# Layer 1's attention: the third and fourth rows of probabilities turned in 32x32 blocks by VectorE and DMA, and values multiplied in blocks of 128 columns, a head later

## The chip, the cores and the metric

The kernel runs on one core of a Trainium2 chip. The metric is the device time of one execution in microseconds. The kernel before takes 2954.98 us (median of three runs, 2953.38 to 2958.42). The engines are named as in the profile: PE (TensorE, matrix products), PEld (its weight loads, which overlap PE), DVE (VectorE), ACT (ScalarE), POOL (GpSimd) and SP (SyncE, which here only issues DMAs). Each engine works through its own list of instructions in order, and waits on semaphores for the others.

## The reference, cut to what matters

Four layers run one after the other, each the sum of an attention-like and a feed-forward part, on 4 sequences of 512 tokens with 256 features. The change lies in the attention of layer 1, a latent attention with 16 heads:

```python
q = _rmsnorm(x @ wq_a, q_a_ln_w) @ wq_b
q_nope, q_pe = (q[..., :D_NOPE], q[..., D_NOPE:])
compressed_kv, k_pe = (ckv[..., :KV_LORA], ckv[..., KV_LORA:])
...
scores = jnp.einsum('bqhd,bkhd->bhqk', qf, kf) * softmax_scale
scores = jnp.where(causal[None, None], scores, jnp.finfo(scores.dtype).min)
attn = jax.nn.softmax(scores, axis=-1)
out = jnp.einsum('bhqk,bkhd->bqhd', attn, v)
return out.reshape(b, s, N_HEADS * D_V) @ wo
```

The mask is causal: of a head's 4 x 4 blocks of 128 queries by 128 keys, ten are computed, one in the first row of blocks, four in the last.

## The kernel before

Layer 1 is one generator, `latent_pieces`, woven with three others: the product-key layer (`product_key_pieces`, with its gathers on POOL), the gated units of the feed-forward part, and the start of the next layer. `weave` takes at each turn the piece that is least advanced by the costs the generators yield; the Tile scheduler then sets the order of the instructions on each engine, and semaphores and buffers follow from that order. Where the code says `keep_in_program_order`, the scheduler keeps the instructions of that engine as they are written.

The weights are folded so that keys and values of all heads are the same 64 latent columns (`cv`) and a head's query has 128 rows: 64 latent ones and 64 rotated ones. There are 64 heads in all (4 sequences by 16), numbered `s`; two make a pair `p = s // 2`. A pair's queries come from `queries` (L1049 to L1074): four matmuls, ScalarE copies of the results, and four DMAs on SP (L1068) that copy the rotary half `pes` into `psw` with its 32-row parts exchanged. `rotate` (L1075 to L1080) then multiplies by cosines and sines and adds, on VectorE, into `qf`.

For each head, and each row i of 128 queries:

- `exp_scores` (L964): one matmul of (i + 1) x 128 columns into a PSUM bank of the tag `mm` (four banks; L971); VectorE adds the mask and finds the row's extreme (L974); ScalarE takes the exponential and the row's sum (L978). The result is the tile `pr0` to `pr3`, of two buffers each.
- At the third and fourth row VectorE inverts the sums (L1094) and ScalarE scales the rows, three at once and then the last (L1096).
- `turned` (L1098, matmuls L1103): for the head before, column block j of all rows from j on is transposed by PE into a PSUM bank of the tag `tr` (two banks), 4, 3, 2 and 1 blocks; VectorE copies even j, ScalarE odd j, into `PT` (L1107), which holds 1280 columns.

After the second head of a pair has been turned, `z` (L1239) is computed: for each column block j and both heads one matmul with `cv` as weights (64 columns, so that the two heads fill two halves of PE's columns) and 512, 384, 256 or 128 columns of `PT`. ScalarE scales `z` into `zT` (L1245), and every second pair two PSUM banks of outputs are formed (L1253) and added to x by VectorE (L171).

In layer 3's attention (`full_attention`), rows are already turned otherwise: VectorE transposes within 32x32 blocks (`turn_blocks`, L1581), four DMAs write the strips to memory (L1586), one reads them back in the final order (L1590), and the values are multiplied in blocks of 128 columns (L1625). Its rows in the profile are therefore rows for the same operations.

Of the kernel before, what the change touches and what calls it, by code (L numbers as in the profile page):

```python
# [16 lines left out]
P = 128  # L17
NB, SEQ, DM = 4, 512, 256
NT = NB * SEQ
NTILE = NT // P  # L20
TPB = SEQ // P
# [9 lines left out]
class Ctx:  # L31


    def __init__(self, tc, stack):
# [8 lines left out]
        self.trickle = []  # L43
# [8 lines left out]
    def unit(self, src, kept=lambda ins: ins):  # L52

        w = self.tile(self.weights, [P, 3072], "wu")
        kept(self.nc.sync.dma_start(w[:, : src.shape[1]], src))
        return w

# [942 lines left out]
def latent_pieces(c, a, keep, open_pool):  # L1000
# [4 lines left out]
    nc, tc = c.nc, c.tc  # L1005
    QL, KL = 192, 64
# [68 lines left out]
    def rotate(pes, psw, qf):  # L1075
        pec = c.tile(pool, [P, SEQ], "pec", bufs=1)
        nc.vector.tensor_mul(pec, pes, cosq)
        tc.keep_in_program_order(nc.vector.tensor_mul(psw, psw, sinq))
        nc.vector.tensor_add(qf[:KL, 1, :], pec[:KL, :], psw[:KL, :])
        nc.vector.tensor_add(qf[KL:, 0, :], pec[KL:, :], psw[KL:, :])  # L1080

    def probabilities(s, i):
        p, h = s // 2, s % 2
        b = p // 2 % 4
        if i == 0:
# [3 lines left out]
            c, pool, late, qfs[p][:, h, :], kf[:, h, b * SEQ : (b + 1) * SEQ], i, rinv[:, i : i + 1]  # L1089
# [8 lines left out]
    def turned(s, j):  # L1098

        pt = c.ps("tr")  # L1100
        n = SEQ - j * P
        for i in range(j, TPB):
            nc.tensor.transpose(  # L1103
                pt[:, (i - j) * P : (i - j + 1) * P], prs[s][i][:, j * P : (j + 1) * P], c.ident
            )
        copy = nc.scalar.copy if j % 2 else nc.vector.tensor_copy
        return lambda: copy(PTs[s][:, START[j] : START[j] + n], pt[:, :n])  # L1107

    START = (0, 512, 896, 1152)
# [5 lines left out]
    def latents(b):  # L1115

        if b < 2:
            rooms = [c.tile(pool, [P, 1280], "PT")[:, :1024]]
        elif b == 2:
            rooms = [c.tile(pool, [P, SEQ], "zT", bufs=3) for _ in range(2)]  # L1120
# [38 lines left out]
    for b in range(NB):  # L1159
        tokens = slice(b * SEQ, (b + 1) * SEQ)  # L1160
        lats.append(latents(b))
        for t in range(TPB):
# [5 lines left out]
            sq = c.tile(pool, [P, QL + KL], "pr1")  # L1168
# [12 lines left out]
        rot = c.tile(pool, [P, SEQ], "pr3")  # L1181
# [22 lines left out]
    copy = None  # L1204
    yield 1.9
    for s in range(65):
        if s < 64:
            prs[s] = []
        for i in range(TPB):
            if s < 64:  # L1210
                probabilities(s, i)
            if s > 0:
                if i == 0:
                    PTs[s - 1] = c.tile(pool, [P, 1280], "PT")
                ready, copy = copy, turned(s - 1, i)
                if ready:
                    ready()
            if i == 0 and s % 2 == 1 and s < 63:
                rotate(*turning)
            yield 0.85  # L1220
            if i == 1 and s % 2 == 0 and s < 62:
                turning = queries(s // 2 + 1)
                yield 2.6
        if copy:
            copy()
            copy = None
        if s > 0:
            del prs[s - 1]
        if s % 2 == 1:
            continue  # L1230
        if s == 0:
            continue

        p = s // 2 - 1
        g, b, pair = p // 8, p // 2 % 4, p % 2
        z = c.ps("acc")
        for j in range(TPB):
            for h in range(2):
                tc.keep_in_program_order(nc.tensor.matmul(  # L1239
                    z[h * KL : (h + 1) * KL, j * P :], lhsT=cv[:, b * TPB + j, :],  # L1240
                    rhs=PTs[s - 2 + h][:, START[j] : START[j] + SEQ - j * P],
                    start=(j == 0), stop=(j == TPB - 1),
                ))
        zTs[pair] = c.tile(pool, [P, SEQ], "zT", bufs=3)
        nc.scalar.mul(zTs[pair], z, kv_w)  # L1245
        yield 2.1
        if pair == 1:
            wz = weights[g][4]
            for t in range(0, TPB, 2):
# [10 lines left out]
                yield 1.7  # L1260

# [133 lines left out]
def layer1(c, a, xn, following):  # L1395


    with ExitStack() as stack, ExitStack() as right:
# [7 lines left out]
        latent = latent_pieces(c, a, keep, lambda: pool_of("l_h", 2))  # L1406
# [985 lines left out]
```

## Time and profile before

| | us |
|---|---|
| median of 3 runs | 2954.98 |
| the profiled execution | 2964.84 |
| its span, first to last instruction | 2962.9 |
| PE busy in the span | 2901.4 (98%) |
| DVE busy | 2136.9 (72%) |
| ACT busy | 1391.0 (47%) |
| layer 1's heads, about | 852 to 1482 |

The busy time of PE counts a matmul from its start to its modelled end; matmuls are pipelined, so successive ones overlap and the step from one start to the next is shorter than the duration shown. A matmul of 32-bit floats leaves two records, a transpose one. "Idle before" is the time for which an engine waited ahead of a group's instructions, with what ended the wait. A long idle time of an engine other than the bound costs nothing by itself. DMA rows give the median time from issue to landing.

### The profile page before, as it was taken

What the parts mean: (1) busy time and instruction counts of PE and PEld (TensorE: products, weight loads), DVE (VectorE), ACT (ScalarE), POOL (GpSimd) and SP (SyncE); (2) the same over time, 40 slices, a digit from 0 to 9 for tenths busy, and PEclk for the clock granted to TensorE, in tenths of its full rate; (3) what the DMA queues carried; (4) which work ended last, traced back from release to release, by engine and by line L of the source; (5) the groups of instructions that cost most, each with busy time, mean ns of one, the idle gap of its engine ahead of it and who ended that gap; (6) DMA issues with size and microseconds to landing.
All of it is one profiled execution on the core that took longest, in us unless ns stands there. A gap on an engine that the chain in (4) does not pass through costs nothing.

```text
span 2962.9 us, 40601 instructions
## 1 busy us (share of the span) xinstructions
PE 2901.4 (98%) x13812; PEld 1958.1 (66%) x13812; DVE 2136.9 (72%) x5434; ACT 1391.0 (47%) x3336; POOL 856.4 (29%) x681
## 2 busy tenths in 40 slices
PE   8999999999999999999999999999999999999999
PEld 5566666666755655555677678888888756666666
DVE  5877778787788788878666877777677666666656
ACT  4444445454376666667624554454454233333332
POOL 0565665656410033332043200000000033333331
PEclk9999999999999999999999999999999899999999
DMA  3333332332320134434244444444444300000000
GB/s 128 104 102 119 101 106 95 108 124 73 113 67 17 54 108 125 119 98 101 81 123 139 138 123 118 137 130 131 130 125 137 102 1 22 22 22 22 22 1 29
DMA packets 138366, 268.03 MB, mean 90 GB/s; under 512 B 19664, under 2 KB 99040, under 8 KB 133808
## 3 DMA queue, kind: packets, MB, share of 16 engines
q1 hardware_dynamic: 123696, 217.65, 23.5%
q0 software_dynamic: 14176, 47.01, 6.2%
q8 instruction: 109, 1.79, 0.2%
q14 instruction: 97, 0.79, 0.1%
q10 hardware_dynamic: 288, 0.79, 0.1%
HBM read 202.21 MB, written 54.26 MB: 87 GB/s over the span
## 4 chain that ended last, share of the span: by engine, by line
PE 81%; DVE 8%; ACT 3%; DMA 3%; POOL 1%; issue 1%; SPq 0%; ACTq 0%; DVEq 0%; POOLq 0%
PE mm L315 15%; PE mm L147 15%; PE mm L971 7%; PE acc L315 6%; PE tr L315 5%; PE acc L1625 5%; PE acc L987 4%; PE tr L809 3%; PE mm L155 2%; PE acc L1239 2%; PE acc L225 2%; PE tr L225 2%; PE acc L787 2%; PE acc L1253 2%; PE tr L1103 2%; DMA PT<-turned 1%
## 5 line engine op out<-in xcount | busy, mean ns | idle before, releaser
L978 ACT ACTIVATE pr<-pr,nm 128x128 f32<-128x128 f32 (+3 forms) x512 | 286.2, 559 | 334.8 <-DVE nm L974 332.7
L974 DVE CUSTOM_DVE_ANT_0 pr<-mm,late 128x128 f32<-128x128 f32 (+3 forms) x512 | 246.3, 484 | 79.0 <-PE mm L971 75.3
L147 PE MATMUL mm<-xnT,wu 128*128 128x512 f32 x624 | 289.1, 601 | 0.0
L326 ACT COPY part<-mm 128x512 f32<-128x512 f32 (+1 forms) x372 | 176.8, 479 | 198.1 <-PE mm L315 189.1
L315 PE MATMUL mm<-token_sums,unit_sums 128*128 128x512 f32 (+1 forms) x624 | 267.7, 512 | 2.1 <-ACT part L326 1.4
L1357 POOL DMA_INDIRECT e<-in_p_experts,ids x128 | 130.0, 1016 | 465.4 <-DVE x L165 325.1
L147 PE MATMUL mm<-xnT,w_in 128*128 128x512 f32 x512 | 229.2, 593 | 0.6 <-DVE cy L577 0.6
L477 DVE SCALAR_TENSOR_TENSOR x<-acc,cw,x 128x128 f32<-128x128 f32 x372 | 128.8, 346 | 107.4 <-PE acc L315 105.9
L577 DVE SCALAR_TENSOR_TENSOR cy<-mm,ws,cy 128x509 f32<-128x509 f32 (+2 forms) x216 | 160.2, 744 | 51.7 <-ACT cy L573 47.7
L147 PEld LDWEIGHTS mm<-xnT,wu 128*128 128x128 f32 x624 | 115.9, 193 | 118.7 <-issue 110.7
L971 PE MATMUL mm<-k,q 128*128 128x128 f32 (+3 forms) x512 | 175.2, 447 | 6.1 <-DVE q L1525 3.4
L971 PE MATMUL mm<-kf,qf 128*128 128x128 f32 (+3 forms) x512 | 173.8, 442 | 3.9 <-DVE qf L1080 3.6
L747 POOL TENSOR_TENSOR G<-G,CB 128x1024 f32<-128x1024 f32 x64 | 151.5, 2367 | 82.7 <-DVE G L710 76.6
L730 ACT ACTIVATE xD<-xc,ws 128x128 f32<-128x128 f32 x256 | 83.9, 390 | 192.7 <-POOL y L771 183.4
L315 PEld LDWEIGHTS acc<-down_sums,hidden_sums 128*128 128x128 f32 x744 | 112.1, 192 | 85.1 <-issue 83.2
L147 PEld LDWEIGHTS mm<-xnT,w_in 128*128 128x128 f32 x512 | 96.5, 190 | 104.4 <-issue 94.9
L1625 PEld LDWEIGHTS acc<-PT,V 128*128 128x128 f32 x1280 | 153.9, 194 | 13.6 <-DMA PT<-turned 9.4
L1625 PE MATMUL acc<-PT,V 128*128 128x128 f32 x1280 | 156.2, 278 | 5.0 <-DMA PT<-turned 4.8
L261 POOL TENSOR_TENSOR down_sums<-wu 128x256 f32<-128x256 f32 x8 | 6.1, 757 | 534.2 <-DMA turned<-Y 425.8
L710 DVE TENSOR_TENSOR_SCAN G<-G,eye 128x1024 f32<-128x1024 f32 x64 | 148.2, 2315 | 0.0
L460 DVE TENSOR_TENSOR whole<-mm,part 128x512 f32<-128x512 f32 x128 | 88.6, 692 | 68.4 <-PE mm L315 67.5
L1103 PEld LDWEIGHTS tr<-con,pr 128*128 128x128 f32 x640 | 79.7, 142 | 82.8 <-issue 20.0
(437 smaller groups left out, 6757.4 us busy)
## 6 DMA issues: line engine op xcount, KB each, us to landing
turned<-Y SPq DMA_DIRECT2D x252, 160.0 KB, 2.6
PT<-turned SPq DMA_DIRECT2D x63, 640.0 KB, 3.9
G<-own SPq DMA_DIRECT2D x64, 512.0 KB, 4.2
w_in<-in_m_units SPq DMA_DIRECT2D x16, 1024.0 KB, 4.9
eb<-since SPq DMA_DIRECT2D x96, 128.0 KB, 3.2
wu<-in_o_units SPq DMA_DIRECT2D x6, 1536.0 KB
wo<-in_m_units SPq DMA_DIRECT2D x16, 512.0 KB, 12.8
psw<-pes SPq DMA_DIRECT2D x128, 64.0 KB, 2.9
```

The costliest lines, as they stand in the source:

```text
L147: c.nc.tensor.matmul(out, lhsT=w[:, d, cols], rhs=c.xnT[:, d, tokens], start=(d == 0), stop=(d == 1))
L315: self.c.tc.keep_in_program_order(self.c.nc.tensor.matmul(bank, lhsT=lhsT, rhs=rhs, start=first, stop=True, skip_group_check=not first))
L326: self.c.nc.scalar.copy(r, bank)
L577: nc.vector.scalar_tensor_tensor(y[:, j:], src[:, : SEQ - j], conv[:, k, 3 - j : 4 - j], y[:, j:], ALU.mult, ALU.add,)
L710: tc.keep_in_program_order(nc.vector.tensor_tensor_scan(flat, flat, eye.rearrange("p h t -> p (h t)"), 0.0, ALU.mult, ALU.add))
L747: nc.gpsimd.tensor_mul(G, G, seqs[b][2][:, t, :][:, None, :].to_broadcast([P, HG, P]))
L971: kept(nc.tensor.matmul(sc, lhsT=q[:, i * P : n], rhs=k[:, :n], start=True, stop=True))
L974: nc.vector.tensor_tensor_reduce(out=pr, in0=sc, in1=late[:, SEQ - n :], scale=scale, scalar=-NEG, op0=ALU.add, op1=ALU.min, accum_out=nm,)
L978: nc.scalar.activation(pr, pr, AF.Exp, bias=nm, scale=-1.0, accum_out=total)
L1103: nc.tensor.transpose(pt[:, (i - j) * P : (i - j + 1) * P], prs[s][i][:, j * P : (j + 1) * P], c.ident)
L1357: nc.gpsimd.indirect_dma_start(out=e, out_offset=None, in_=a["p_experts"], in_offset=bass.IndirectOffsetOnAxis(ap=ids[:, t, k : k + 1], ax ...
L1625: kept(nc.tensor.matmul(zs[:, i], lhsT=head["V"][:, j, h, :], rhs=head["PT"][:, :, i * (i + 1) // 2 + j, :], start=(j == 0), stop=(j == i),))
```

## The change

- The third and fourth rows of a head (`i >= 2`, all heads but the last) are no longer transposed by PE. `turn_strips` has VectorE transpose each row within 32x32 blocks into one tile `Y` (one buffer, 896 columns); after the fourth row four DMAs on SP write its four 32-row strips to a memory tile `strips` (two buffers), and a fifth reads them back into the first 896 columns of `PT`, so that whole 128x128 blocks stand transposed. The new `chain` keeps these DMAs of SP in their written order among themselves.
- The first and second rows are transposed by PE (three blocks, one PSUM bank) at the end of their own head; ScalarE copies them into the last 384 columns of `PT` at the start of the next.
- The last head has its third and fourth rows transposed by PE, one bank each.
- The values of a pair are a function `values`, called in the third row of the second head after that pair's last (`s % 2 == 1`, `s > 2`), and run over blocks of 128 queries by 128 keys: 20 matmuls of 128 columns for a pair instead of 8 of 128 to 512. Blocks of rows three and four are read with a stride, four strips of 32.
- To make room: `pr0` to `pr3` have one buffer, not two; `zT` two, not three; `PT` three; the rotation multiplies in place and the tile `pec` is gone. The latents' scratch tiles move to `Y` and a single-buffered `pr1`.

```diff
     def rotate(pes, psw, qf):
-        pec = c.tile(pool, [P, SEQ], "pec", bufs=1)
-        nc.vector.tensor_mul(pec, pes, cosq)
+        nc.vector.tensor_mul(pes, pes, cosq)
...
-    def turned(s, j):
-        pt = c.ps("tr")
-        n = SEQ - j * P
-        for i in range(j, TPB):
-            nc.tensor.transpose(
-                pt[:, (i - j) * P : (i - j + 1) * P], prs[s][i][:, j * P : (j + 1) * P], c.ident
-            )
-        copy = nc.scalar.copy if j % 2 else nc.vector.tensor_copy
-        return lambda: copy(PTs[s][:, START[j] : START[j] + n], pt[:, :n])
+    def strips(ap):
+        return ap.rearrange("p (j a s) -> p j a s", a=4, s=32)
+    def wide(tile, i):
+        lo = 0 if i == 2 else 3
+        return tile[:, :896].rearrange("p (a j s) -> p j a s", j=7, s=32)[:, lo : lo + i + 1]
+    def turn_strips(s, i):
+        if i == 2:
+            Ys[s] = c.tile(pool, [P, 896], "Y", bufs=1)
+        nc.vector.transpose(wide(Ys[s], i), strips(prs[s][i]))
+        if i == TPB - 1:
+            room = c.tile(dram, [4, 32, 4, 224], "strips")
+            PTs[s] = c.tile(pool, [P, 1280], "PT", bufs=3)
+            Y = Ys.pop(s)
+            for a in range(4):
+                c.chain(nc.sync.dma_start(
+                    room[:, :, a, :].rearrange("b r e -> r b e"),
+                    Y[a * 32 : (a + 1) * 32].rearrange("p (b e) -> p b e", b=4),
+                ))
+            c.chain(nc.sync.dma_start(PTs[s][:, :896], room.rearrange("b r a e -> (b r) (a e)")))
+    def turned(s, rows):
+        if s not in PTs:
+            PTs[s] = c.tile(pool, [P, 1280], "PT", bufs=3)
+        pt, n = c.ps("tr"), 0
+        for i in rows:
+            for j in range(i + 1):
+                nc.tensor.transpose(
+                    pt[:, n * P : (n + 1) * P], prs[s][i][:, j * P : (j + 1) * P], c.ident
+                )
+                n += 1
+        if rows[0] == 0:
+            return lambda: nc.scalar.copy(PTs[s][:, 896:], pt[:, : 3 * P])
+        return lambda: nc.scalar.copy(wide(PTs[s], rows[0]), strips(pt[:, : n * P]))
...
+    def block(s, i, j):
+        if i < 2:
+            lo = 896 + (i + j) * P
+            return PTs[s][:, lo : lo + P]
+        return wide(PTs[s], i)[:, j]
...
+    def values(p):
         g, b, pair = p // 8, p // 2 % 4, p % 2
         z = c.ps("acc")
-        for j in range(TPB):
-            for h in range(2):
-                tc.keep_in_program_order(nc.tensor.matmul(
-                    z[h * KL : (h + 1) * KL, j * P :], lhsT=cv[:, b * TPB + j, :],
-                    rhs=PTs[s - 2 + h][:, START[j] : START[j] + SEQ - j * P],
-                    start=(j == 0), stop=(j == TPB - 1),
-                ))
+        for i in range(TPB):
+            for j in range(i + 1):
+                for h in range(2):
+                    tc.keep_in_program_order(nc.tensor.matmul(
+                        z[h * KL : (h + 1) * KL, i * P : (i + 1) * P], lhsT=cv[:, b * TPB + j, :],
+                        rhs=block(2 * p + h, i, j), start=(j == 0), stop=(j == i),
+                    ))
...
+    for s in range(66):
+        if s < 64:
+            prs[s] = []
+        for i in range(TPB):
+            if s < 64:
+                probabilities(s, i)
+                if i >= 2 and s < 63:
+                    turn_strips(s, i)
+            if copy:
+                copy()
+                copy = None
+            if s < 64 and i == TPB - 1:
+                copy = turned(s, (0, 1))
+            if s == 64 and i < 2:
+                copy = turned(63, (i + 2,))
+            if i == 0 and s % 2 == 1 and s < 63:
+                rotate(*turning)
+            yield 0.85
+            if i == 1 and s % 2 == 0 and s < 62:
+                turning = queries(s // 2 + 1)
+                yield 2.6
+            if i == 2 and s % 2 == 1 and s > 2:
+                yield from values(s // 2 - 1)
```

## The prediction

> **What bounds the kernel now.** I read the page's busy shares first, then the stretch in which layer 1's attention runs, cut into four, then that stretch's groups of instructions by shape, and last the timeline of single heads.
>
> Busy time by stretch; the columns are the stretch and its length, then busy us (and instructions) of PE, PEld, DVE, ACT and POOL, the granted clock, the DMA share and GB/s:
>
> ```profile
> 850.00:1000.00 150.00, 145.62 (x655) 84.95 (x654) 119.91 (x444) 96.47 (x260) 0.00 (x0) 0.99 0.13 37
> 1000.00:1200.00 200.00, 197.37 (x886) 113.28 (x885) 164.13 (x567) 137.97 (x371) 57.23 (x56) 1.00 0.41 108
> 1200.00:1400.00 200.00, 193.17 (x857) 111.21 (x857) 162.65 (x552) 133.51 (x357) 65.20 (x65) 0.99 0.42 107
> 1400.00:1482.00 82.00, 80.19 (x392) 52.53 (x391) 53.52 (x183) 51.59 (x125) 0.55 (x1) 0.94 0.21 73
> 850.00:1482.00 632.00, 616.35 (x2787) 361.96 (x2787) 500.21 (x1743) 419.53 (x1110) 122.97 (x122) 0.99 0.32 86
> ```
>
> TensorE is busy 616 of 632 us: it is the bound. VectorE, at 500 us (79%, 82% between 1000 and 1200), stands close behind, and DMA moves 86 GB/s.
>
> The groups of that stretch that the change touches (busy us, mean ns | idle before, and what ended it):
>
> ```profile
> L1103 PE MATMUL tr<-con,pr 128*128 128x128 f32 x640 | 116.3, 281 | 8.4 <-ACT PT L1107 3.0 <-DVE PT L1107 2.0 <-ACT pr L1096 1.9
> L1107 DVE COPY PT<-tr 128x512 f32<-128x512 f32 x64 | 43.9, 686 | 28.9 <-PE tr L1103 28.8
> L1107 DVE COPY PT<-tr 128x256 f32<-128x256 f32 x64 | 26.3, 412 | 6.2 <-PE tr L1103 6.2
> L1107 ACT COPY PT<-tr 128x384 f32<-128x384 f32 x64 | 30.4, 475 | 30.3 <-PE tr L1103 29.4
> L1107 ACT COPY PT<-tr 128x128 f32<-128x128 f32 x64 | 16.3, 254 | 13.7 <-PE tr L1103 13.4
> L1078 DVE TENSOR_TENSOR psw<-psw,tab 128x512 f32<-128x512 f32 x32 | 22.0, 687 | 12.1 <-DMA psw<-pes 11.6 <-issue 0.5
> ```
>
> Layer 3's attention already turns probabilities by VectorE and DMA; its rows price the new operations:
>
> ```profile
> L1581 DVE STREAM_TRANSPOSE Y<-pr 128x512 f32<-128x512 f32 x63 | 44.5, 706 | 0.5
> L1581 DVE STREAM_TRANSPOSE Y<-pr 128x384 f32<-128x384 f32 x63 | 36.2, 575 | 1.8
> turned<-Y SPq DMA_DIRECT2D x252, 160.0 KB, 2.6
> PT<-turned SPq DMA_DIRECT2D x63, 640.0 KB, 3.9
> ```
>
> The timeline gives the pace of PE (start, length, count of records) and one head's chain from scores to scaled rows:
>
> ```profile
> 1217.17 0.93 PE L1103 MATMUL tr<-con,pr 128*128 128x128 f32 x7
> 1225.30 0.39 PE L1239 MATMUL acc<-PT,cv 128*64 128x128 f32 x4
> 1661.69 2.39 PE L1625 MATMUL acc<-PT,V 128*128 128x128 f32 x20
> ...
> 1212.57 1.02 PE L971 MATMUL mm<-kf,qf 128*128 128x512 f32 x2
> 1213.63 0.69 DVE L974 CUSTOM_DVE_ANT_0 pr<-mm,late 128x512 f32<-128x512 f32 x1
> 1214.37 0.72 ACT L978 ACTIVATE pr<-pr,nm 128x512 f32<-128x512 f32 x1 [0.15 <-DVE nm L974]
> 1215.09 1.90 ACT L1096 ACTIVATE pr<-pr,total 128x128 f32<-128x128 f32 x4
> ```
>
> Seven transposes take 0.93 us, and the last alone is 0.27, so one follows the other after (0.93 - 0.27)/6 = 0.11 us, not after the 281 ns of its row. From the start of the fourth row's scores (1212.57) to the end of the first row's scaling (1215.09 + 0.39) are 2.9 us.
>
> **The change part by part** (in the stage; PE decides unless said).
>
> 1. *Transposes removed.* Before, 64 heads x 10 = 640. After, 63 x 3 + 10 = 199. Gone: 441 x 0.11 = -48.5 us. The row's busy time (116.3/640 = 0.18 each) would make it -80, but it counts tails that the next matmul covers; I take -48.5.
>
> [...]
>
> 2. *Waits at the removed transposes.* Of the 8.4 us of PE idle in their row, 5.0 ended on a PSUM copy; four copies a head become one. -4 (between 0 and -8).
>
> 3. *Values by 128 columns.* Same columns, but 20 matmuls a pair of heads for 8, and strips of 32 for contiguous rows. Layer 3's values read such strips at (2.39 - 0.27)/19 = 0.11 us a step. Two heads write two halves of the columns: four records of 128 columns took 0.39 us, that is two steps, side by side. So 20 steps and a tail, 2.5 us for 2.37 shown for a pair at 1223.32: 32 x 0.12 = +4. Not side by side it would be 40 steps, +2.1 each, +66; the four records speak against it.
>
> 4. *VectorE and ScalarE.* VectorE loses two copies (686 + 412) and gains two block transposes (575 + 706): 63 x 0.18 = +11.5 us. ScalarE loses 254 ns a head, -16. Both lie beside PE: VectorE has 632 - 500 = 132 us idle. If that cover were gone, +11.5. Its waits for PE's transposes (35.0 of the two rows) go; in their place it waits for ScalarE's scaling. In the built order 21 of 63 heads have under 2.4 us of VectorE work between the fourth row's reduction and the first block transpose; their shortfalls add up to 22 us. About even: 0. The in-place rotation waits one multiplication sooner for the same DMAs: 0.
>
> 5. *Rows one and two are transposed in their own head, not a head later, from one buffer.* In the built order the PE work between the start of the fourth row's scores and the first transpose falls from a median of 4.65 to 2.7 us. Against the chain of 2.9 us, 36 heads fall short by 28.6 us in sum (before: 5 heads, 4.3): +24. Behind that wait stand on PE the next head's scores, and on VectorE the next head's first row, which cannot be written before the transpose has read it. If VectorE comes to the fourth row a microsecond late, the same count against 3.9 us gives 73.3 - 18.2 = +55; if the scaling is early, 0.
>
> 6. *Values wait for the strips.* The odd head's chain: reduction 0.8, VectorE work up to the second block transpose (1.7 to 10.1 us by the order, at least 3.1 for the scaling), that transpose 0.7, then from the first strip's issue to the load's issue 4.1 (layer 3's median), issue 0.3, landing 3.9. Against PE's work up to the first value matmul that needs it, stretched by the stage's pace (about 0.88 of it streaming), 14 of 31 pairs fall short, by 40 us in sum. Waits of point 5 lie inside the same distance and lengthen it; layer 3 waits 14.2 us for its like. I take +20, between 0 and +40.
>
> 7. *The queues.* SP issues five DMAs a head more (315 in all; 4 x 0.44 + 0.34 us). The rotation's four copies (L1068) share that queue: in the built order the last of the four stands behind the load, which waits for the strips to land; the three before it are issued meanwhile, so it comes 0.5 to 0.8 us later. The load of 448 KB and strips of 112 KB add 63 x 0.92 MB = 58 MB, some 92 GB/s to the 86. The copies land after 2.4 us (median) in the window 852 to 1010, at a low DMA share, and 3.3 at 0.43 (1040 to 1440): another 0.9. Together up to 1.7 us on 31 pairs, +53; 10 of 31 had no slack before, and 8.5 us of PE's waits ended on that rotation's output where VectorE had waited 11.6, so 10 x 1.3 x 0.7 = +9, taken as +8. Lower end 0. The POOL queue gets nothing new; its gathers share the engines but VectorE waits only 1.1 us for them now. The key and token loads on SP that wait for VectorE stand, in the order, behind work that precedes the next head's block transposes: 0.
>
> Sum: -48.5 - 4 + 4 + 0 + 24 + 20 + 8 = +3.5 us on a span of 2962.9. The profiled execution took 2964.84, which is 9.9 (0.33%) above the median of the runs, 2954.98; the difference is carried over: 2954.98 + 3.5 = 2958.5, say 2959.
>
> **The rivals.**
> - *The gain is kept.* If the waits of 5 to 7 fall into one another (all three are one lateness of PE) and cost only half, 26 instead of 52: -48.5 + 26 = -22.5; with almost none, -45. For it: PE is the bound, and layer 3 works this way at 695 busy of 710 us. Against: layer 3's order is written out; here the scheduler put the transposes close behind the scores. 2910 to 2940, centre 2930.
> - *The strips come late (slower).* One mechanism: DMA under gathers. If strips and load land 1.5 us later each, another 3 us on the 14 short pairs and about 1 on the others, +59 at most, half of it real: +30 on the sum, about 2988. It decides once the strips' chain exceeds some 9 us from first issue to landing (8.3 in layer 3).
> - *VectorE becomes the bound.* It needs 512 us. Between 1000 and 1400 it would have 327 + 42 x 0.18 = 334 us in a stretch that PE could do in 400 - 42 x 0.77 = 368: 91%, more than any 100 us show now. If it manages 85%, that stretch takes 393 and gains 7; the rest gains 10 at most; with points 3 and 7 about 2950.
>
> **How the numbers follow.** Even give-and-take 0.40 (2945 to 2975, centre 2959; a quarter of it faster by over 0.2%, a third within, the rest slower); the gain kept 0.25; VectorE the bound 0.10 (half faster, the rest split evenly); strips late 0.25. 0.2% is 6 us, about what a measurement of this kernel can tell from no change. Faster: 0.25 + 0.10 + 0.05 = 0.40. Within: 0.13 + 0.02 = 0.15. Slower: 0.25 + 0.17 + 0.03 = 0.45. The range leaves out one tenth on each side: 2915 (almost none of the waits) to 3000 (late strips and the upper ends of 5).
>
> **What would show it.** Right: 199 transposes, PE busy in the stage's groups down by 48 us or more, and in return PE and weight-load waits on the scaling (some 30 us), on the loaded strips (15 to 25), and VectorE at or above 80%. Block transposes at 0.57 and 0.71 us; values at 2.5 us a pair. Wrong: waits at the values under 10 us and at the scaling under 15 mean the gain stays; a strip landing over 3.5 us or value pairs at 4.5 us mean a plain loss.

## The result, and the profile after

The changed kernel takes 3030.77 us (median of four runs, 3026.75 to 3033.57), the kernel before in the same session 2954.18: a ratio of 1.0252, interval 1.0235 to 1.0269. It is 2.5% slower; 2959 was forecast, and 3000 was the end of the range. The profiled execution took 3033.57 us, its span 3031.8.

All of it lies in the stage that was changed. From the first matmul of its scores to the last of its outputs it went from 852.7–1481.9 (629.2 us) to 856.1–1559.4 (703.3 us), 74 us more. Busy time by stretch after (stretch and length, busy us and instructions of PE, PEld, DVE, ACT, POOL, granted clock, DMA share, GB/s):

```profile
850.00:1000.00 150.00, 129.38 (x649) 77.70 (x648) 115.80 (x430) 89.27 (x234) 0.00 (x0) 0.95 0.41 114
1000.00:1200.00 200.00, 176.31 (x887) 106.79 (x888) 144.38 (x472) 114.80 (x293) 40.56 (x40) 0.95 0.62 167
1200.00:1400.00 200.00, 175.51 (x864) 106.70 (x863) 151.96 (x491) 115.52 (x298) 64.08 (x64) 0.93 0.69 185
1400.00:1560.00 160.00, 139.19 (x742) 90.20 (x742) 109.76 (x364) 96.17 (x229) 17.06 (x19) 0.91 0.55 158
856.10:1559.40 703.30, 614.36 (x3099) 376.80 (x3099) 516.23 (x1737) 412.27 (x1045) 121.70 (x122) 0.94 0.58 160
```

The same row of before:

```profile
852.70:1481.90 629.20, 613.68 (x2773) 360.05 (x2772) 497.46 (x1738) 418.14 (x1107) 122.97 (x122) 0.99 0.32 87
```

Before, PE was busy 613.68 of 629.20 us at a clock of 0.99. Now it is busy for the same 614 us, though 441 transposes are gone, and idle for 89 instead of 16. Two things are to be seen: PE waits, and its clock is lower (0.94). Where it is low, matmuls last longer: behind PE's longest wait for strips, at a clock of 0.50, the same records of the values last 425 ns on average instead of 280 (last section). So less work can take the same time. VectorE, at 516 of 703 us (73%), is further from being the bound than it was.

The groups of the stage that answer to those shown of before:

```profile
L1145 PE MATMUL tr<-con,pr 128*128 128x128 f32 x199 | 46.8, 312 | 21.4 <-ACT pr L1109 20.5
L1262 PE MATMUL acc<-PT,cv 128*64 128x128 f32 x1280 | 107.2, 305 | 28.0 <-DMA PT<-strips 28.0
L1126 DVE STREAM_TRANSPOSE Y<-pr 128x512 f32<-128x512 f32 x63 | 43.2, 685 | 0.1
L1126 DVE STREAM_TRANSPOSE Y<-pr 128x384 f32<-128x384 f32 x63 | 36.1, 572 | 9.4 <-DMA strips<-Y 6.0 <-ACT pr L1109 2.2 <-ACT pr L991 1.2
L1150 ACT COPY PT<-tr 128x384 f32<-128x384 f32 x64 | 29.6, 462 | 0.5 <-PE tr L1145 0.4
```

The prices are the forecast ones: 199 transposes, block transposes of 0.57 and 0.69 us. What PE waits for in the stage (us in total, times, longest):

```profile
PE acc L1262 <- DMA PT<-strips: 28.0, 10, 5.6
PE tr L1145 <- ACT pr L1109: 20.5, 19, 3.6
PE mm L984 <- DVE qf L1092: 18.0, 12, 2.9
PE acc L1277 <- ACT zT L1269: 7.7, 9, 1.3
```

The loaded strips, the scaled rows, the rotated queries and the scaled values, in that order. One passage of the timeline has PE's longest wait for strips, and VectorE's for the rotation's copies beside it:

```profile
1075.87 0.59 ACT L1079 COPY pes<-mm 128x512 f32<-128x512 f32 x1
1076.39 2.30 SPq L1132 DMA_DIRECT2D strips<-Y  x4
1078.73 1.78 SPq L1081 DMA_DIRECT2D psw<-pes  x3
1083.06 0.34 SPq L1136 DMA_DIRECT2D PT<-strips  x1
1083.45 0.77 SPq L1081 DMA_DIRECT2D psw<-pes  x1
1090.88 2.40 PE L1262 MATMUL acc<-PT,cv 128*64 128x128 f32 x20 [5.62 <-DMA PT<-strips]
1091.59 0.69 DVE L1089 TENSOR_TENSOR pes<-pes,tab 128x512 f32<-128x512 f32 x1 [4.02 <-DMA psw<-pes]
```

The strips are issued until 1078.69, their load only at 1083.06, when they have landed, and PE gets the strips at 1090.88, 7.8 us after that. The rotation's copies, whose input was there at 1076.46, stand behind both on SP: the fourth goes out at 1083.45, and VectorE starts the rotation at 1091.59. From this page alone the strips look like the cause. The runs say otherwise.

### The profile page after: what moved, and what is told of

It is laid out like the page before. It is cut to its first block, busy times and chain, and to the rows that moved or that the text cites. A ratio compares the mean times of both kernels' runs of the same rounds, so it can differ in the third digit from the quotient of the medians.

```text
span 3031.8 us, 41980 instructions
## 1 busy us (share of the span) xinstructions
PE 2900.4 (96%) x14139; PEld 1973.4 (65%) x14139; DVE 2156.2 (71%) x5432; ACT 1385.8 (46%) x3274; POOL 854.9 (28%) x681
## 3 DMA queue, kind: packets, MB, share of 16 engines
q1 hardware_dynamic: 169056, 275.47, 29.5%
## 4 chain that ended last, share of the span: by engine, by line
PE 78%; DVE 10%; DMA 5%; ACT 3%; issue 2%; POOL 2%; SPq 1%; DVEq 0%; ACTq 0%; POOLq 0%
PE mm L328 15%; PE mm L160 14%; PE mm L984 6%; PE acc L328 6%; PE tr L328 5%; PE acc L1681 4%; PE acc L1000 4%; PE tr L822 3%; PE mm L168 2%; PE tr L238 2%; PE acc L800 2%; PE acc L1262 2%; PE acc L1277 2%; DMA strips<-Y 2%; DMA PT<-strips 2%
## 5 line engine op out<-in xcount | busy, mean ns | idle before, releaser
L984 PEld LDWEIGHTS mm<-kf,qf 128*128 128x128 f32 x512 | 86.4, 195 | 78.9 <-issue 22.9
```

Source lines behind the costliest of these rows:

```text
L984: kept(nc.tensor.matmul(sc, lhsT=q[:, i * P : n], rhs=k[:, :n], start=True, stop=True))
```

## The experiments

Each time below is a ratio to the kernel before, measured in the same session on the same chip. The chips differ: on two of them the kernel before takes about 3025 to 3032 us, on the others 2951 to 2954; the table marks the first B, the second A. "Idle" is the stage's length less PE's busy time, in one profile. Stage rows of A and B are not to be compared to the microsecond: on B engines have waits that the profile puts down to nothing in the core (last section). In the stage VectorE has 10 us of them in e1, 15 in e5, 37 in e6 and in e18. The kernel before was not profiled on B.

| run | what | ratio | chip | stage us | PE busy | idle | clock |
|---|---|---|---|---|---|---|---|
| before | | 1 | A | 629.2 | 613.7 | 15.5 | 0.99 |
| after | | 1.0252 | A | 703.3 | 614.4 | 88.9 | 0.94 |
| e5 | after again | 1.0275 | B | 734.8 | 624.0 | 110.8 | 0.92 |
| e1 | no DMAs | 1.0010 | B | 651.0 | 591.7 | 59.4 | 0.97 |
| e6 | DMAs, data not awaited | 1.0299 | B | 745.6 | 617.5 | 128.1 | 0.91 |
| e18 | as e6, load moved | 1.0281 | B | 731.1 | 617.1 | 114.0 | 0.92 |
| e10 | as e6, 1/14 of the bytes | 0.9992 | A | 621.5 | 584.2 | 37.3 | 0.98 |
| e11 | as e6, no load | 1.0075 | A | 649.2 | 597.0 | 52.2 | 0.95 |
| e13 | no DMAs, free traffic | 1.0083 | A | 647.8 | 590.4 | 57.4 | 0.96 |
| e12 | before, free traffic | 1.0103 | A | 653.2 | 621.8 | 31.3 | 0.98 |
| e16 | as e6, rotation by PE | 0.9989 | A | 619.3 | 594.8 | 24.5 | 0.99 |
| e14 | after, rotation by PE | 1.0128 | A | 660.9 | 618.0 | 42.9 | 0.97 |

**e1_nodma: are the DMAs the cause?** The block transposes stay, the five DMAs a head go, and the values read `Y` where it lies (four buffers of it).

```diff
-            for a in range(4):
-                c.chain(nc.sync.dma_start(room[:, :, a, :]..., Y[a * 32 : (a + 1) * 32]...))
-            c.chain(nc.sync.dma_start(PTs[s][:, :896], room.rearrange("b r a e -> (b r) (a e)")))
...
-        return wide(PTs[s], i)[:, j]
+        return wide(Ys[s], i)[:, j]
```

> The changed kernel without its strip DMAs: VectorE turns the blocks as before, but the five DMAs of a head are left out and the values read Y itself (four buffers of Y, the first two rows in a small PT), so the blocks of rows three and four stand in the wrong order and the output is wrong there; every other instruction stays. Theory A (late strips: the values wait for the DMA chain, and its traffic delays the rotation's copies): the waits of PE on the load (28 us, 36 at the weight loads) and most of those on the rotated queries (18 us) go; 2940 to 2965. Theory B (the transposes and single buffers of a head bind its own scaling): PE still waits for the scaling, 3005 to 3025. Both in part: about 2985.

3027.9 us against 3026.5 for the kernel before on that chip, 1.0010 (0.9995 to 1.0026). The whole loss comes with the five DMAs (that it isn't the other buffers of this kernel, e6 shows, which has them too); but without the DMAs the kernel is no faster than before either.

**e2_pswact: the rotation's copies on ScalarE's queue.**

```diff
-            nc.sync.dma_start(psw[to : to + 32, :], pes[to ^ 32 : (to ^ 32) + 32, :])
+            nc.scalar.dma_start(psw[to : to + 32, :], pes[to ^ 32 : (to ^ 32) + 32, :])
```

> The changed kernel with the four copies of the rotary half issued on ScalarE's queue instead of SP's, so that they no longer stand behind the strips and the load. Theory A1 (the place in SP's queue makes the rotation late): PE's waits on the rotated queries (18 us at matmuls, 22 at weight loads) fall by more than half, 3005 to 3018. Theory A2 (the traffic makes them late, the queue does not matter): 3025 to 3035, and ScalarE busier by some 50 us of issuing.

1.0211 (1.0150 to 1.0273). The time is some half a per cent under e5's, with intervals that overlap; PE's waits for the rotated queries at matmuls, 18.2 us, did not fall by half, as A1 wanted. VectorE now waits 28.6 us for the copies, and ScalarE itself 14.1, so the move brings costs of its own.

**e3_trlater: the first two rows transposed a head later**, as before the change, from two buffers of `pr0` and `pr1`.

```diff
-            if s < 64 and i == TPB - 1:
-                copy = turned(s, (0, 1))
+            if 0 < s < 65 and i == 0:
+                copy = turned(s - 1, (0, 1))
```

> The changed kernel with the first and second rows transposed a head later, as before the change, from two buffers of pr0 and pr1 (room made by one buffer of wl0 instead of two). Theory B (transposes in their own head wait for the scaling, and the next head's first row waits for them): PE's waits on the scaling (20 us, 43 at the weight loads) and VectorE's on those transposes (24 us) go, 2995 to 3010. Theory A: PE then waits at the values instead, 3020 to 3030.

1.0267 (1.0202 to 1.0332): no help. PE still waits 26.4 us for the scaled rows, though the transposes stand further behind the scaling.

**e4_before128: the kernel before with values by 128 columns**, the other half of the change alone.

```diff
-        for j in range(TPB):
+        for i in range(TPB):
+            for j in range(i + 1):
```

> The kernel before with its values in blocks of 128 columns (20 matmuls a pair for 8), nothing else changed. Side by side as in the prediction (+4 us): 2955 to 2962. If the two halves of the columns no longer run side by side, or the small matmuls disturb the order: 2985 to 3020.

1.0053 (1.0019 to 1.0087), some 16 us, between the two forecasts. Yet a pair's values take 2.40 us in its timeline against 2.37 before. What the other 15 us are, no run settles; the interval begins at 6.

**e5_after_again** is the changed kernel again, beside the next three.

> The changed kernel itself once more, as the level for the three that run beside it, since the chip of the last runs was some 2.4% slower for every kernel. All theories: 1.025 times the kernel before (1.0235 to 1.0269 measured first).

1.0275 (1.0239 to 1.0310).

**e6_traffic: the same DMAs, but nobody waits for their data.** e1's kernel, with the four strips and the load issued where the change has them; the load goes from memory to memory.

```diff
+            for a in range(4):
+                c.chain(nc.sync.dma_start(room[:, :, a, :]..., Ys[s][a * 32 : (a + 1) * 32]...))
+            c.chain(nc.sync.dma_start(back.rearrange(...), room.rearrange(...)))
```

> The kernel without waits for strips (VectorE's blocks are read from Y directly, wrong order in rows three and four), but with the five DMAs of a head issued again on SP at the same place and of the same size; the fifth writes to memory instead of PT, and no engine waits for its data. Theory A (the values wait for the landing): about the kernel before, 0.998 to 1.006 of it. Theory A3 (the traffic and SP's queue, through later rotation copies and gathers, are what costs): 1.015 to 1.025 of it.

1.0299 (1.0258 to 1.0339): the full loss, although the values wait for no strip. PE's waits in its stage:

```profile
PE mm L984 <- DVE qf L1092: 57.2, 16, 8.3
PE tr L1148 <- ACT pr L1109: 30.2, 17, 6.8
```

The wait for strips is gone and PE waits longer for the rotated queries instead (18.0 us in the changed kernel, 26.1 in e5). So the wait at the values doesn't carry the loss. But VectorE, which makes the rotated queries, hardly waits for a DMA either. These are all its waits for DMAs in e6's stage:

```profile
DVE prod L1425 <- DMA e<-in_p_experts,ids: 4.6, 3, 3.1
DVE Y L1126 <- DMA strips<-Y: 1.7, 2, 1.0
DVE pes L1089 <- DMA psw<-pes: 1.2, 1, 1.2
```

They are 7.5 us, 1.2 of them for the rotation's copies; in the kernel before they are 12.8 and 11.6. PE and ScalarE wait for no DMA at all here. The traffic costs 3.0%, and hardly any of it by data that come late to an engine.

**e7_nodma_trlater: e1 and e3 together.**

> The kernel without strip DMAs (wrong order in rows three and four) and with rows one and two transposed a head later from two buffers of pr0 and pr1. Theory B (what is left of the loss without the DMAs is the wait for the scaling in the head's own transposes and the single buffers): faster than the kernel before by 20 to 40 us, 0.987 to 0.994 of it. If the lost gain lies elsewhere (order of the values, VectorE, single buffers of the last two rows): 0.998 to 1.003.

0.9979 (0.9959 to 0.9999). Without the DMAs, moving the transposes gains 0.3% on e1, about 9 us, far less than the forecast 20 to 40. Since the two intervals overlap, this is a rough price of the short distance from scaling to transposes.

**e8_valsrow: the values one row later.**

```diff
-            if i == 2 and s % 2 == 1 and s > 2:
+            if i == 3 and s % 2 == 1 and s > 2:
```

> The changed kernel with the values called one row later (in the fourth row of the second head after the pair, ahead of that head's block transposes), correct. Theory A (the values stand too close behind the strips): PE's waits on the load fall by half and the time by 15 to 35 us against the changed kernel. If the distance was only a symptom of a lateness shared by all (VectorE and scaling): within 8 us of the changed kernel.

1.0273 (1.0233 to 1.0313), e5's ratio. PE still waits 29.2 us for strips: a later place of the values doesn't take the wait away. The time is what was expected if the distance is only a symptom of a lateness shared by all.

**e9 to e12: bytes, or the place on SP?** e9 is e6 with the rotation's copies on ScalarE's queue (e2's line).

> The kernel of the run with the five DMAs whose data nobody waits for (its ratio to before was 1.030), and besides the rotation's four copies are issued on ScalarE's queue instead of SP's. Left out as there: the loaded strips are not used, so rows three and four of the values are wrong. Now nobody that computes waits for anything on SP behind the strips. Theory 'queue' (the copies stand behind strips and the load that waits for the strips' landing): the ratio falls to 1.000-1.010 and PE's waits for rotated queries from 57 us to under 20. Theory 'contention' (the bytes slow every transfer, the copies and the gathers too): 1.020 or more, and the waits for queries or for ScalarE stay above 40 us. Issuing on ScalarE itself costs 32 x 4 x 0.6 us = 77 us of that engine, which has some 290 us to spare in the stage; it may add up to 0.5%.

1.0229 (1.0204 to 1.0255). The ratio is the one of 'contention'; PE's wait for rotated queries at matmuls, 12.8 us, is the one of 'queue'. VectorE waits 35.0 us for copies that nothing on SP holds up, and ScalarE's score rows wait 12.8 us behind the copies that it issues.

```diff
# e10_traffic_small, on e6
-                    Ys[s][a * 32 : (a + 1) * 32].rearrange("p (b e) -> p b e", b=4),
+                    Ys[s][a * 32 : (a + 1) * 32].rearrange("p (b e) -> p b e", b=4)[:, :, :16],
```

> The kernel of the run with the five DMAs whose data nobody waits for, with each DMA at the same place and with as many rows, but 16 of 224 elements of a row: 8 KB a strip for 112 and 32 KB for 448, a fourteenth of the bytes. Left out: rows three and four of the values are wrong, as there. Theory 'contention': ratio 1.000-1.008, DMA share of the stage about .35 instead of .56. Theory 'queue' (issues and the load's wait in SP's order): 1.020-1.030 stays, since the number of issues and the wait for a landing remain; the landing of a small strip is perhaps 2 us instead of 4, which would take a third off.

0.9992 (0.9979 to 1.0005), against 'queue': 315 issues with their waits on SP cost nothing when the transfers are small.

e11 is e6 without the load:

> The kernel of the run with the five DMAs whose data nobody waits for, without the fifth: four strips a head are written, nothing is loaded, so nothing on SP waits for a landing. Left out: rows three and four of the values are wrong, as there. Theory 'queue': ratio 1.000-1.010, because the copies behind the load no longer wait. Theory 'contention': half the bytes and four fifths of the rows remain, so 1.012-1.022.

1.0075 (1.0057 to 1.0093). Half the bytes, a quarter of the loss. By its number this is the forecast of 'queue'; e17 and e18 test that theory by itself.

```diff
# e12_before_traffic, on the kernel before, after the fourth row's scores
+                    for q in range(4):
+                        c.chain(nc.sync.dma_start(room[:, :, q, :]..., tab[q * 32 : (q + 1) * 32, :896]...))
+                    c.chain(nc.sync.dma_start(back, a["l_units"][0][:, :896]))
```

> The kernel before, all of it, with five more DMAs a head on SP after the fourth row's scores: four of 112 KB from the rotation's table to memory in the strips' layout and one of 448 KB from weights in memory to memory. None waits for the head's data, none waits for another of the same head, nobody waits for them: bytes and issues alone. Theory 'contention': ratio 1.015-1.03, the rotation's copies land later (VectorE's wait for them above 25 us instead of 12, PE's for the queries above 20 instead of 9). Theory 'queue': at most 1.005, the issues alone (2.1 us a head of SP, which is nearly idle).

1.0103 (1.0086 to 1.0120). Between the two forecasts, so bytes alone slow even the kernel before. The issue rows of the stretch 852 to 1480 (size, median us from issue to landing), of before and then of e12:

```profile
psw<-pes SPq DMA_DIRECT2D x124, 64.0 KB, 2.9
e<-in_p_experts,ids POOLq DMA_INDIRECT x120, 4.3
```

```profile
psw<-pes SPq DMA_DIRECT2D x124, 64.0 KB, 3.8
e<-in_p_experts,ids POOLq DMA_INDIRECT x120, 8.0
```

The copies land 0.9 us later and the gathers 3.7. VectorE's wait for the copies rises from 11.6 to 24.7 us, and the one for the gathers from 1.1 to 18.6.

**e13_free_traffic: bytes, or the planned order?** The scheduler sets each engine's order before the run, and it plans with the transfers: the order with full bytes (e6) is not that with small ones (e10). e13 puts e12's free traffic into e1's kernel, whose order stays nearly what it was.

> The kernel of the run without the five DMAs (block transposes kept, nothing read back; its ratio to before was 1.001), with the free traffic of the last run of before: four DMAs of 112 KB and one of 448 KB a head on SP, from constants to memory, which wait for no result and which nobody waits for. Left out as there: rows three and four of the values are wrong. The planned order of TensorE differs from the run without the DMAs in 151 of 5159 lines and from the run with the heads' own traffic in 346; VectorE's in 496 and 2095 of 5324. Theory 'bytes' (contention): ratio 1.012-1.030, as the bytes alone cost 1.0% in before, and this program has less slack for the rotation's copies. Theory 'order' (the scheduler, which plans with the transfers, chose a worse order, and the bytes cost what they cost in before): at most 1.011 = 1.001 + 0.010.

1.0083 (1.0064 to 1.0102): below the forecast for 'bytes', inside the one for 'order'. The bytes cost about what they cost in the kernel before, 0.7 to 1.0%, and here the engines do wait for late data:

```profile
DVE prod L1423 <- DMA e<-in_p_experts,ids: 29.3, 28, 3.0
DVE pes L1089 <- DMA psw<-pes: 13.8, 9, 4.4
```

The heads' own traffic costs three times as much (e6), with 7.5 us of such waits.

**e14 to e16: without the rotation's copies.** One matmul with a permuted identity swaps the halves, and VectorE reads PSUM:

```diff
-        for to in range(0, P, 32):
-            nc.sync.dma_start(psw[to : to + 32, :], pes[to ^ 32 : (to ^ 32) + 32, :])
...
+        turning[1] = c.ps()
+        nc.tensor.matmul(turning[1], lhsT=swap, rhs=turning[0], start=True, stop=True)
```

> The changed kernel, with the rotation's swapped halves made by one 128x512 matmul with a permuted identity instead of four DMAs from SBUF to SBUF; VectorE reads the product from PSUM. Nothing is left out. It costs 32 x 0.6 = 19 us of TensorE (0.65%). Theory 'the late copies carry the loss': the queries' waits (18 to 57 us) and VectorE's waits for the copies go, the ratio falls from 1.0275 to 1.005-1.015, under what the matmul costs plus the strips' waits. Theory 'any transfer will do' (gathers, the strips' own landing, the scaling chain): ratio 1.020 or more, with PE's waits for the loaded strips and for VectorE above 50 us.

1.0128 (1.0101 to 1.0155), in the changed kernel.

> The kernel before with the same one matmul in place of the four copies, and the rotation's first product written in place, as the changed kernel does. Nothing is left out. It prices the matmul: 19 us more on TensorE, against 8.5 us of its waits for rotated queries and 11.6 of VectorE's for the copies: ratio 1.002-1.007. A gain would need the copies' waits to cost more than they show.

1.0060 (1.0039 to 1.0082), in the kernel before: the matmul's price, 18 us, less what the copies' waits had cost.

> The kernel with the heads' own traffic whose data nobody waits for (ratio 1.030), with the matmul in place of the rotation's copies. Left out as there: rows three and four of the values are wrong. Now only the gathers and the few loads of the other layers can be late. Theory 'the late copies carry the loss': 1.003-1.010, about the matmul's price. Theory 'any transfer will do': 1.015 or more, with VectorE's waits for the gathers above 30 us.

0.9989 (0.9977 to 1.0001), in e6's kernel. This is the clearest contrast of the study: with the copies, the heads' own traffic costs 3.0%; without them, with the matmuls added and at a DMA share of 0.64, nothing. It is not a pair in every respect: e6 ran on B and e16 on A (the changed kernel's ratio differs by 0.2% between them), and the planned order changed with the copies (table below). The stage of e16, and its two longest waits on PE:

```profile
851.12:1470.46 619.34, 594.81 (x3157) 364.61 (x3157) 509.99 (x1739) 409.83 (x1042) 121.82 (x122) 0.99 0.64 168
```

```profile
PE mm L984 <- DVE nm L987: 8.5, 11, 2.0
PE tr L1155 <- ACT pr L1116: 4.3, 9, 2.0
```

In e14 the waits for strips and for scaled rows fall with it, from 28.0 and 20.5 us to 6.6 and 5.5, though nothing about strips or scaling was changed. But e14 and e16, measured on one chip, are 1.4% apart (about 41 us). In e14 the values wait for the strips, and `Y` has one buffer instead of four. So with the rotation's copies gone, using the strips does cost something; by which of the two, no run tells.

**e17 and e18: the place on SP behind the load.** In the planned order 30 fourth copies stood directly behind a load that waits for strips to land. Here an odd head's load is put behind all four copies, in the changed kernel (e17) and in e6's (e18), by making the copies part of SP's chain as well.

```diff
+            if i == 1 and s % 2 == 0 and 0 < s < 63:
+                load(s - 1)
```

> The changed kernel, with one thing moved: in the planned order of SP the load of an odd head stands behind the rotation's four copies instead of ahead of the fourth (30 of 32 fourth copies stood directly behind a load that waits for the strips to land; now none). Nothing is left out, the same bytes, TensorE's order differs in 250 of 5170 lines. Theory 'queue' (a copy waits behind the load's wait): the ratio falls from 1.0275 to 1.008-1.018, what is left being the bytes (0.8%) and the waits for strips and scaling. Theory 'bytes and pace' (the copies are late through contention wherever they stand): 1.022 or more.

1.0238 (1.0195 to 1.0281): not the range of 'queue'.

> The kernel with the heads' own traffic whose data nobody waits for (ratio 1.030), with the same move: an odd head's load behind the rotation's four copies. Left out as there: rows three and four of the values are wrong. TensorE's planned order differs in 83 of 5159 lines, the bytes are the same. Theory 'queue': 1.006-1.014, about what free traffic costs (1.008). Theory 'bytes and pace': 1.022 or more.

1.0281 (1.0241 to 1.0322). In e18 the last copy is out 2.50 us after its input is there (median; before 2.44, after 3.97), and the loss stays. The place behind the load is not the cause; nor are late copies, as 'bytes and pace' had it. What is seen instead is this passage of e18's timeline:

```profile
1063.09 1.32 DVE L1126 STREAM_TRANSPOSE Y<-pr 128x384 f32<-128x384 f32 x2 [1.03 <-ACT pr L1109]
1064.34 0.65 DVE L192 SCALAR_TENSOR_TENSOR sg<-sg,mm 128x512 f32<-128x512 f32 x1
1064.91 0.67 DVE L1089 TENSOR_TENSOR pes<-pes,tab 128x512 f32<-128x512 f32 x1
1065.51 0.68 DVE L1090 TENSOR_TENSOR psw<-psw,tab 128x512 f32<-128x512 f32 x1
1066.10 0.68 DVE L193 SCALAR_TENSOR_TENSOR hT<-sg,mm 128x512 f32<-128x512 f32 x1
1066.70 0.68 DVE L1091 TENSOR_TENSOR qf<-pes,psw 64x512 f32<-64x512 f32 x1
1067.39 0.69 DVE L1092 TENSOR_TENSOR qf<-pes,psw 64x512 f32<-64x512 f32 x1
1068.14 1.61 PE L984 MATMUL mm<-kf,qf 128*128 128x128 f32 x4 [4.16 <-DVE qf L1092]
```

VectorE doesn't wait for a copy here (in the whole stage of e18, 0.0 us). It comes to the rotation late: in its planned order the rotation stands behind block transposes that wait for the scaling, and PE has nothing left to do but the new pair's scores. This can be counted in the planned order, before any run: the score rows that PE has multiplied before the new queries' first use, less those that VectorE has reduced before its last addition to them. It is the number of rows between the finished rotation and its use:

| kernel | median rows | of 31 pairs with none | ratio |
|---|---|---|---|
| before; e12 (free traffic) | 3; 3 | 2; 1 | 1; 1.0103 |
| e1; e10; e13 (no DMAs, small, free) | 1; 1; 1 | 0; 0; 6 | 1.0010; 0.9992; 1.0083 |
| e11 (no load) | 1 | 12 | 1.0075 |
| after; e6; e17; e18 | 0; 0; 0; 0 | 24; 19; 19; 20 | 1.0252; 1.0299; 1.0238; 1.0281 |
| e3; e8 (transposes, values later) | 0; 0 | 24; 28 | 1.0267; 1.0273 |
| e2; e9 (copies on ScalarE's queue) | 3; 3 | 0; 0 | 1.0211; 1.0229 |
| e14; e16 (rotation by PE) | 3; 3 | 0; 0 | 1.0128; 0.9989 |

With the heads' own traffic in the plan, the rotation moves to the last moment. In e6, 54.2 of the 57.2 us that PE waits for rotated queries fall on the 19 pairs with none; in e18 it is 36.9 of 41.8, in the changed kernel 10.4 of 18.0. In e17 it is only 1.1 of 13.4: there PE waits for the scaled rows instead (41.6 us). The two runs on ScalarE's queue break the pattern: there the place is early again, and VectorE then waits for the copies themselves (28.6 us in e2, 35.0 in e9).

**What is shown and what stays open.** Shown: the loss comes with the five DMAs (e1), grows with their bytes (e10, e11), needs nobody to wait for their data (e6), and is gone from e6's kernel when the rotation needs no copies (e16). Not the cause: the copies' place behind the load (e17, e18), the transposes' distance (e3), and, in e6 and e18, data that land late, since the engines wait 7.5 and 5.7 us for them, less than the 12.8 of before. Bytes by themselves make 0.7 to 1.0 of the 2.5 to 2.75% (e12, e13). What fits the rest is the planned order, which puts the rotation at the last moment when the heads' own traffic is in the plan. This is argued from the count above and from who waits for whom, not shown: in e10, e11 and e16 the order changed together with the traffic or the copies, and e13 and e6 differ in the chip besides. A run with e6's traffic in e1's order, which would tell, was not tried. Also open are what e14 loses beyond its matmul, and why the kernel without the DMAs is no faster than before. None of the kernels that leave nothing out is faster than the kernel before.

## Why the prediction was wrong

*How the miss divides.* In the stage +3.5 us was forecast and +74.1 measured. PE's idle time was to grow by 48 us (steps 2, 5, 6 and 7) and grew by 73.4; its busy time was to fall by 44.5 (steps 1 and 3) and rose by 0.7. So 25 us of the miss are longer waits, and 45 are a gain that PE's busy time doesn't show. The sum has no term for the second: it charges a wait with its length alone, and the clock fell from 0.99 to 0.94.

*Step 7, the queues, is the step that failed*: +8, with +53 as its upper end. What the five DMAs cost is e5 less e1: 1.0275 - 1.0010 = 2.65% of 2954, 78 us, where steps 6 and 7 together had 28. Step 7 knew one way from the DMAs to a loss: a copy lands late, VectorE waits for it, PE waits for VectorE. In the changed kernel VectorE waits 8.4 us for copies, less than the 11.6 of before, and yet PE's wait for the rotated queries grew by 14.4 us, from this row of before to the 18.0 shown above:

```profile
PE mm L971 <- DVE qf L1080: 3.6, 2, 3.3
```

In e6, with 1.2 us of waits for copies, it is 57.2. The price was charged to the "10 of 31" pairs that "had no slack before"; in 10 places VectorE had waited for a copy. That belonged to the old order, in which 2 of 31 pairs have no score row between the finished rotation and its use. In the order of the changed kernel, which could be read before the run, it is 24 of 31. The landing was taken at 0.9 us more (measured at a DMA share of 0.43); e12 shows 0.9 more at its median, so that part was right for free traffic.

*Without steps 6 and 7* the forecast is -24.5 us. e1, which has neither the DMAs nor a wait for them, measured +3. So part of the gain was missing before any transfer: step 3 took 12 us more than forecast (below), and the rest is not assigned.

*Step 1, transposes removed, -48.5*: the count is right (199). Where the transfers are small (e10) PE's busy time in the stage is 584.2 us against 613.7, 29.5 less; if e4's 16 us for the narrower values are all PE's, that makes 45. So by this estimate the work did go. In the changed kernel it can't be seen. If busy time goes as one over the clock, another estimate, 0.94 stretches what is left to 584.2 x 0.98 / 0.94 = 609 of the 614.4 us.

*Step 2, waits at the removed transposes, -4*: the waits for PSUM copies, 5.0 us, are gone from the rows. Right, and small.

*Step 3, values by 128 columns, +4*: 2.5 us a pair forecast, 2.40 measured, but the kernel before with this alone loses 16 us (6 to 26). The pair's time was right and the step's cost too low.

*Step 4, VectorE and ScalarE, 0*: durations right; VectorE's busy time rose by 19 us (497.5 to 516.2), not 11.5, but its share fell. The rival *VectorE becomes the bound* is out.

*Step 5, rows transposed in their own head, +24*: PE waits 20.5 us there, near the forecast, but by itself the step is worth 9 us (e7 less e1), and with the DMAs it is not additive (e3).

*Step 6, values wait for the strips, +20*: measured 28.0, inside its bounds. But e6 shows that taking this wait away gains nothing as long as the rotation is late; e14 against e16 leaves room for a cost where it isn't late. To add steps 5, 6 and 7 was itself doubtful: with one wait gone another grows (e6, e17), as the rival *the gain is kept* said with its one lateness. It concluded that the sum must be smaller; what came was larger.

*The strips come late*, about 2988, had the sign, and there is more traffic under the gathers (they land after 6.2 us in the changed kernel, 4.3 before). Its channel was wrong: without any wait for the strips' landing (e6) the loss is the same.

What the list of signs was worth: waits at the values (28.0 us at the matmuls) and at the scaling (20.5) came near what stands under *right*, and the time did not. Such waits go with a loss of 75 us as well as with none. Two signs failed: PE's busy time "down by 48 us or more" (up by 0.7), and VectorE "at or above 80%" (73%). Both pointed the right way: no engine was the bound any more.

## What to carry to other kernels

Slack belongs to an order, not to a kernel: when a change adds transfers, count again in the new planned order how much work lies between each small transfer's consumer and the use of its result, and charge lateness to all pairs that have none. The wait that is longest in the profile may only be where lateness shows; make the same transfers without anyone waiting for them, and the time tells at once. Then look how long any engine waits for a transfer: where that is little (7.5 us in e6, 5.7 in e18), late data are not the reason. A wait on TensorE may cost more than its length: behind one of 5.62 us the clock was 0.50 for 3.1 us. And the heavy traffic was free only where the rotation no longer needed transfers and nobody waited for the strips (e16, 0.9989); with the strips in use it still cost 1.3% (e14).

## What the runs showed of the hardware

*PE's granted clock is lower mostly where PE idles.* Stretches of 20 us of the changed kernel around the passage shown above:

```profile
1060.00:1080.00 20.00, 18.41 (x102) 9.86 (x101) 16.33 (x52) 14.38 (x39) 4.79 (x5) 1.00 0.48 133
1080.00:1100.00 20.00, 14.20 (x66) 9.55 (x68) 10.54 (x30) 7.67 (x19) 3.03 (x4) 0.83 0.61 167
1100.00:1120.00 20.00, 18.23 (x88) 9.24 (x85) 18.41 (x66) 15.13 (x40) 8.19 (x8) 1.00 0.80 205
```

Of its 35 such stretches from 860 to 1560, 23 have PE busy under 18 us, and 15 of these a clock under 0.95; of the other 12, four have. In the kernel before one of 31 (860 to 1480) is busy under 18 us, at 0.91. The tie is not exact: from 1540 to 1560, after a stretch with 14.2 us of busy time, PE is busy throughout at 0.71. The stretch at 0.83 is the one with the 5.62 us wait for strips, which ends at 1090.88. From 1091.0 to 1094.1 PE is busy throughout and the clock is 0.50; in the 5.9 us after that it is 0.98. The 26 records of the values behind the wait last 425 ns on average, the 54 from 1060 to 1080 last 280; the 20 shown in the passage above take 2.40 us, as long as a pair's 40 do in e4. So this wait cost more than its length.

*On two of the chips engines stop now and then.* In every profile from the chips marked B, and in none from the others, engines have waits that the profile calls `remote`, since nothing in the core's records ends them, about 105 to 150 us in sum over all engines. Two of VectorE's in e1:

```profile
DVE p_half L1849 <- remote: 23.6, 1, 23.6
DVE pr L987 <- remote: 10.1, 3, 4.6
```

There the kernel before takes 2.4% longer (3026 against 2954 us). What these waits are, and whether they are all of the 2.4%, the records don't show. Ratios nearly stand up to it (1.0252 and 1.0275 for the changed kernel), times across chips do not.
